# A perceiver block: the maximum of a softmax found in 32x32 blocks on VectorE and one small transposition on TensorE

## The chip, the core and the metric

The kernel runs on one core of a Trainium2 chip. TensorE (PE) multiplies matrices into PSUM, VectorE (DVE) and ScalarE (ACT) work elementwise, GpSimd (POOL) adds and issues some loads, SyncE (SP) issues the others. The metric is the device time of one launch in microseconds, a median of several runs; less is better. Granted TensorE clock in the profiled execution: 1.000.

## What is computed

Eight batches of 64 latent rows of 512 pass through cross attention on a context of 1601 rows of 256 per batch (16 heads of 128), causal self attention, and a gated feed-forward layer with ternary weights, each with a residual. The change lies in the softmax of the cross attention:

```python
q = (hidden_states @ Wq).reshape(B, Sq, H, D)
k = (encoder_hidden_states @ Wk).reshape(B, Skv, H, D)
v = (encoder_hidden_states @ Wv).reshape(B, Skv, H, D)
q = rmsnorm(q, gq)
k = rmsnorm(k, gk)
scores = jnp.einsum('bqhd,bkhd->bhqk', q, k) * scale
attn = jax.nn.softmax(scores, axis=-1)
out = jnp.einsum('bhqk,bkhd->bqhd', attn, v)
```

With `B` = 8, `Sq` = 64, `Skv` = 1601, `H` = 16, `D` = 128.

## The kernel before

**Units.** The cross attention is cut into 16 units: unit `u` is one batch and one half of the heads (8 heads of 64 queries, so 512 columns, `W`). Scores lie with the keys on the partitions: 12 full tiles of 128 keys and a tail of 65, each 128 x 512. The keys are never projected for the scores: the query side is multiplied with the key weights ahead of the loop, and the context itself is the other factor. The projected keys are needed only for their norms: squares are summed, and each row of scores is scaled by the root.

**Steps.** A unit has six steps, `step(u, q)`, q from 0 to 5, with two key tiles each (a pair). The projected keys and the scores of a pair come from a 2x2 block scheme with seven products instead of eight. `p_u` (tag "k" in PSUM), `p_5` and `p_2` (tag "m") are banks of key products; `s_a` and `s_2` (tag "s") those of scores. `c12`, `c22` and `c11` are sums that VectorE makes out of banks (L963, L981, L1010); ScalarE squares them (L684). The last product of a step into `p_u` overwrites what `c22` has read.

**One unit behind.** While unit `u` makes its scores, unit `u - 1` goes through its softmax: in step 0 its maximum is found, in steps 1 to 4 `less_max` subtracts it on VectorE, `exponentials` runs on ScalarE, `add_to_sums` on GpSimd; `weigh` (L775, `y`) multiplies the exponentials with the context, two tiles per step and three in step 1, three tiles later still (`LAG`); `finish` (L802) divides by the sums in the step in which the last of these products ends. In the first unit that has a predecessor, step 0 has nothing to weigh. `later` holds the scaling of the pair before, with its running maximum (`scale_pair`, L654 and L670), which is run early in the next step.

**The maximum.** `mx[u]`, 128 x 512, holds for every partition the maximum over the 13 tiles. `find_max` turns it on TensorE in four 128x128 transpositions into a bank of tag "m" (`tp_mx`, L733) and reduces over the free axis (L735): `m`, 128 x 4, one maximum per column. To put it on all partitions `spread_diag` splits it into two fp32r parts (L703, L705) and multiplies the identity with each (`dg`, 128 x 512, L709); `spread` sums the rows of both with a matrix of ones (`bp`, L110), and ScalarE copies the bank to `mB` (L727). In step 0 the first two are called behind the exponentials and ahead of `weigh(1)` and `product_7`; `spread_max` is called near the end of the step, behind the last score product.

**Order.** In the loop the order on PE, DVE, ACT and POOL is that of the calls (`tc.manual_schedule`). Behind the loop only PE keeps it; a scheduler orders the other engines. There the last unit's maximum is found, the first half of the values is projected (`values`, `vp`, L846), its exponentials are taken and weighed (`y`).

**Buffers.** Tiles of a tag share that tag's buffers: "t2" has 12 buffers of 128 x 512, "m", "k" and "s" two PSUM banks each.

Of the kernel before, what the change touches and what calls it, by code (L numbers as in the profile page):

```python
# [9 lines left out]
F32 = mybir.dt.float32  # L10
BF = mybir.dt.bfloat16

FR = mybir.dt.float32r
AF = mybir.ActivationFunctionType
ALU = mybir.AluOpType
AX = mybir.AxisListType
# [3 lines left out]
P = 128  # L20
# [8 lines left out]
def perceiver_kernel(  # L29
# [18 lines left out]
    nc = tc.nc  # L48
# [7 lines left out]
    HG = H // G  # L56
# [10 lines left out]
    W = HG * S  # L67
# [11 lines left out]
    small = ctx.enter_context(tc.tile_pool(name="small", bufs=4))  # L79
# [4 lines left out]
    ident = const.tile([P, P], F32, name="ident")  # L84
# [22 lines left out]
    def sum_rows(out_, parts):  # L107

        for i, part in enumerate(parts):
            nc.tensor.matmul(  # L110
                out_, ones_r, part, start=(i == 0), stop=(i == len(parts) - 1)
            )

    def moments(src, t):
# [467 lines left out]

    def quantise(u, aw, sg):

        tot = small.tile([P, 8], F32, tag="tot", name="tot")
        nc.vector.tensor_reduce(tot, aw, AX.X, ALU.add)
        scl = small.tile([P, 8], BF, tag="scl", name="scl")
        nc.vector.tensor_scalar(scl, tot, 1.0 / 64, SCALE_MIN, ALU.mult, ALU.max)

        thr = small.tile([P, 8], F32, tag="thr", name="thr")  # L590
        nc.vector.tensor_scalar(thr, scl, 257.0 / 512, None, ALU.mult)
        m = fq.tile([P, 8, 64], BF, tag="m", name="m")
        nc.vector.tensor_tensor(
            m, aw, thr.unsqueeze(2).to_broadcast([P, 8, 64]), ALU.is_gt
        )
        nd = fq.tile([P, 8, 64], BF, tag="nd", name="nd")
        nc.vector.tensor_tensor(
            nd, aw, scl.unsqueeze(2).to_broadcast([P, 8, 64]), ALU.subtract
        )
        return u, m, nd, aw, sg  # L600
# [71 lines left out]
    def bank(name, tag="m"):  # L672
        return ps.tile([P, 4 * HD], F32, tag=tag, name=name)
# [4 lines left out]
    def product(out_, a, w, start):  # L678

        nc.tensor.matmul(out_, a, w, start=start, stop=True, skip_group_check=not start)  # L680
# [15 lines left out]
            load_context(u, j)  # L696
            n_cx += 1

    def spread_diag(col):


        hi = small.tile([P, W // P], FR, tag="chi", name="chi", bufs=2)
        nc.vector.tensor_copy(hi, col)  # L703
        lo = small.tile([P, W // P], FR, tag="clo", name="clo", bufs=2)
        nc.vector.tensor_tensor(lo, col, hi.bitcast(F32), ALU.subtract)  # L705
        dg = []
        for part in (hi, lo):
            d = work.tile([P, W // P, P], FR, tag="t2", name="dg", bufs=12)
            nc.vector.tensor_tensor(  # L709
                d,  # L710
                ident.unsqueeze(1).to_broadcast([P, W // P, P]),
                part.bitcast(F32).unsqueeze(2).to_broadcast([P, W // P, P]),
                ALU.mult,
            )
            dg.append(d.rearrange("p a k -> p (a k)"))
        return dg

    def spread(parts):

# [4 lines left out]
    def spread_max(u):  # L724
        bp = spread(mB[u])
        mB[u] = work.tile([P, HG, S], F32, tag="t2", name="mB", bufs=12)
        nc.scalar.copy(mB[u].rearrange("p h s -> p (h s)"), bp)  # L727

    def find_max(u):
        tp = bank("tp_mx").rearrange("p (i k) -> p i k", k=P)  # L730
        flat = mx[u].rearrange("p h s -> p (h s)")
        for i in range(W // P):
            nc.tensor.transpose(tp[:, i, :], flat[:, ts(i, P)], ident)  # L733
        m = small.tile([P, W // P], F32, tag="m4", name="m4")
        nc.vector.tensor_reduce(m, tp, AX.X, ALU.max)  # L735
        mB[u] = m

    def tiles_of(u, js):
# [25 lines left out]
    def weigh_context(u, j):  # L764
        b, g = divmod(u, G)
        r = rows(j)
        if j == 0:
            yps[u] = [
                ps.tile([P, HG, S], F32, tag=f"y{c}", name=f"y{c}", bufs=1)
                for c in range(NC)  # L770
            ]
        s = s_sb.pop((u, j))
        s_pair.pop((u, j // 2), None)
        for c in range(NC):
            nc.tensor.matmul(  # L775
                yps[u][c],
                cxn[u, j][:r, ts(c, P)],
                s[:r],
                start=(j == 0),
                stop=(j == NJ - 1),  # L780
            )
# [16 lines left out]
    def finish(u):  # L798

        b, g = divmod(u, G)  # L800
        for c in range(NC):
            nc.vector.tensor_tensor(  # L802
                a_sb[g][c][:, :, ts(b, S)], yps[u][c], rB[u], ALU.mult
            )
# [37 lines left out]
    def values(h, tag):  # L842
        g, hg = divmod(h, HG)
        vp = ps.tile([P, NT], F32, tag=tag, name="vp")
        for c in range(NC):
            nc.tensor.matmul(  # L846
                vp,
                wv_sb[g][:, c, ts(hg, HD)],
                a_sb[g][c][:, hg, :],
                start=(c == 0),  # L850
                stop=(c == NC - 1),
            )
        if g == 0:
            o_sb[h] = work.tile([P, NT], F32, tag="og", name="o_h", bufs=HG)
        else:
            o_sb[h] = work.tile([P, NT], F32, tag="t2", name="o_h", bufs=12)
        (nc.scalar.copy if h % 2 else nc.vector.tensor_copy)(o_sb[h], vp)
# [24 lines left out]
    def weigh(k):  # L882
        nonlocal n_av
        for _ in range(k):
            if n_av >= 0:
                load_contexts(n_av + CXN)
                weigh_context(*divmod(n_av, NJ))
                if n_av % NJ == NJ - 1:
                    finish(n_av // NJ)
            n_av += 1  # L890

    def step(u, q):
# [14 lines left out]

        p_u = bank("p_u", "k")
        product(p_u, a11, b11, True)
        for js in probs[:1]:  # L910
            less_max(u - 1, js)
        if u > 0 and q == NQU - 1 and halves:
# [17 lines left out]
            less_max(u - 1, js)  # L930
        while later:
            later.pop(0)()

        n_early = 1 if q == 4 else 0
        for js in probs[:n_early]:
# [35 lines left out]
            for j in js:  # L971
                add_to_sums(u - 1, j, nc.gpsimd)

        if u > 0 and q == 0:
            find_max(u - 1)
            mB[u - 1] = spread_diag(mB[u - 1])
        c22 = kept("c22")

        def product_7():
# [2 lines left out]

        if u > 0 and q != 1:
            weigh(1)
        if q == NQU - 1 and n_q - 1 in quantised:
            put_by(n_q - 1)
        if u > 0 and q == NQU - 1:
# [16 lines left out]
        product(s_a[:, 1], s3, v3, False)  # L1004
        product(s_a[:, 0], s4, q22, False)
        nc.vector.tensor_tensor(quarters[:, 1::2], s_a, half[:, 0:2], ALU.add)  # L1006
        p_2 = bank("p_2")
        product(p_2, a12, b21, True)
        c11 = kept("c11")
# [7 lines left out]
        product(s_2, a12, q21, True)  # L1017
        nc.vector.tensor_tensor(quarters[:, 0], s_2, half[:, 2], ALU.add)
        product(s_a[:, 1], a22, m4, False)
        if u > 0 and q == 0:  # L1020
            spread_max(u - 1)
        nc.scalar.copy(quarters[:, 2], s_a[:, 1])
        if halves:
            signed(*halves.pop())
# [37 lines left out]
    with tc.manual_schedule(engines={mybir.EngineType.PE}):  # L1062

        later.pop()()
        wv_sb.append(load_wv(1))
        for jw in range(NJ - LAG, NJ):
            load_contexts((last - 1) * NJ + jw + CXN)
            weigh_context(last - 1, jw)
        find_max(last)
        mB[last] = spread_diag(mB[last])  # L1070
        finish(last - 1)
        for h in range(HG // 2):
            values(h, "k")
        spread_max(last)
        for h in range(HG // 2, HG):
            values(h, "k")
        x_sb = wkv.tile([P, NTT, D], F32, tag="w", name="x_again")
        nc.gpsimd.dma_start(x_sb, xf.rearrange("(t p) d -> p t d", p=P))
        for j in range(NJ):
            less_max(last, (j,))  # L1080
            exponentials(last, (j,))
            add_to_sums(last, j, nc.vector)
        n_wo = 0
        for j in range(NJ):
            load_contexts(last * NJ + j + CXN)
            weigh_context(last, j)
            if j == NJ - 3:
                find_sum(last)
            if j == NJ - 2:
                spread_sum(last)  # L1090
                for i in range(4):
                    invert_sums(last, i)
        for h in range(H):
            load_wo(h)
        wa_qk = big.tile([P, ND, 2 * D], F32, tag="A", name="wa_qk")
        nc.gpsimd.dma_start(
            wa_qk, w_attn[:, 0 : 2 * D].rearrange("(c p) n -> p c n", p=P)
        )
        wa_vp = big.tile([P, 2, ND, D], F32, tag="A", name="wa_vp")
        nc.gpsimd.dma_start(  # L1100
            wa_vp[:, 0], w_attn[:, 2 * D :].rearrange("(c p) n -> p c n", p=P)
        )
        nc.gpsimd.dma_start(wa_vp[:, 1], w_aproj.rearrange("(c p) n -> p c n", p=P))
        finish(last)


        x1 = x_sb
        ops = {0: ps.tile([P, D], F32, tag="s", name="op")}
        project(ops[0], 0, range(HG))
        for h in range(HG, H):  # L1110
            values(h, "k")
# [487 lines left out]
```

## Time and profile before

| what | us |
|---|---|
| median of 3 runs (1689.68 to 1690.12) | 1689.89 |
| the profiled execution | 1689.57 |
| its span, first to last instruction | 1687.8 |
| first and last start of `tp_mx` | 206.7 and 1398.0 |
| from one unit's `tp_mx` to the next (602.74 to 682.37) | 79.63 |
| `tp_mx`: 64 matmul records, one | 0.273 |
| L735, reduction of `tp_mx`: 16, one | 0.691 |
| L709, `dg`: 32, one | 0.684 |
| `bp` from `dg`: 32 records, one | 0.488 |
| `mB`, ScalarE's copy: 16, one | 0.578 |

Times of instructions count from the start of the span. A record of a matmul reaches beyond the start of the next, since matmuls are pipelined: the distance of two starts is what TensorE gives to one. In an order of time, a line with "x4" merges four instructions that follow each other, and brackets at its end give the engine's idle time before it and what ended that.

### The profile page before, as it was taken

The numbers are of one execution on the slowest core, as the hardware profiler recorded it, in microseconds if no ns is written. First come the engines' busy times: TensorE is split into PE (matmuls) and PEld (weight loads), VectorE is DVE, ScalarE is ACT, GpSimd is POOL, SyncE is SP. The second block draws the span as 40 slices with busy tenths as digits, with TensorE's granted clock in tenths as the row PEclk, the third lists the DMA queues.
The fourth block names the chain that finished last, engine by engine and source line by source line (L and its number), as shares of the span: only waits on it lengthen the run. The fifth ranks groups of instructions, "written<-read, shape, count | busy, mean of one in ns | idle before, by whom it ended". The sixth has DMA issues, their size and how long they took to land.

```text
span 1687.8 us, 20130 instructions
## 1 busy us (share of the span) xinstructions
PE 1668.6 (99%) x5472; PEld 953.1 (56%) x5472; DVE 1194.6 (71%) x1918; ACT 1155.2 (68%) x4511; POOL 448.1 (27%) x590
## 2 busy tenths in 40 slices
PE   7999899999999999999999999999999999999999
PEld 4665455555555555555555555555555554466787
DVE  4446878787888778787878787878788786245541
ACT  4667787878787877777777878787878773023441
POOL 3211232324232323232322323242324122100040
PEclk9999999999999999999999999999999999999999
DMA  6001122212221222222222222121221216500330
GB/s 200 16 0 36 33 52 45 48 39 50 49 52 36 45 47 49 48 43 47 43 49 47 44 46 47 40 57 43 46 43 37 63 30 238 156 1 1 100 101 25
DMA packets 255977, 92.61 MB, mean 55 GB/s; under 512 B 210144, under 2 KB 236536, under 8 KB 255864
## 3 DMA queue, kind: packets, MB, share of 16 engines
q1 hardware_dynamic: 246426, 69.04, 18.3%
q0 software_dynamic: 8864, 22.02, 4.4%
q8 instruction: 43, 0.70, 0.2%
q14 instruction: 70, 0.57, 0.1%
q10 hardware_dynamic: 574, 0.27, 0.1%
HBM read 77.62 MB, written 7.34 MB: 50 GB/s over the span
## 4 chain that ended last, share of the span: by engine, by line
PE 94%; ACT 3%; DVE 2%; DMA 1%; issue 0%; SPq 0%; DVEq 0%; ACTq 0%
PE y L775 21%; PE p_u L680 19%; PE s_a L680 14%; PE p L680 14%; PE gu L1414 4%; PE op L861 3%; PE s L680 2%; PE fop L1528 2%; PE mm_qk L1209 2%; PE aps L484 2%; PE vp L846 2%; PE sp L633 2%; PE q_u L388 2%; PE kp L266 1%; PE q L388 1%; ACT c L684 1%
## 5 line engine op out<-in xcount | busy, mean ns | idle before, releaser
L684 ACT ACTIVATE c<-c 128x128 f32<-128x128 f32 x1152 | 340.6, 297 | 143.4 <-DVE c L981 57.7
L775 PE MATMUL y<-s,cxn 128*128 128x512 f32 x768 | 356.6, 592 | 0.0
L775 PEld LDWEIGHTS y<-s,cxn 128*128 128x128 f32 x768 | 144.6, 190 | 151.2 <-issue 137.0
L684 ACT ACTIVATION_READ_ACCUMULATOR c<-c 128x1 f32 x1152 | 215.4, 187 | 0.0
L762 POOL TENSOR_TENSOR den<-den,s 128x512 f32<-128x512 f32 x150 | 190.7, 1271 | 43.4 <-ACT s L753 36.4
L680 PEld LDWEIGHTS s_a<-aT,cxS 128*128 128x128 f32 x576 | 109.3, 190 | 138.0 <-issue 126.8
L969 POOL COPY gate<-mx 128x1 f32<-128x1 f32 x60 | 11.0, 183 | 619.0 <-DVE mx L668 287.6
L680 PE MATMUL s_a<-aT,cxS 128*128 128x256 f32 x576 | 171.4, 379 | 0.0
L654 DVE TENSOR_TENSOR s<-s,ssq 128x1024 f32<-128x1024 f32 x96 | 117.2, 1221 | 25.4 <-ACT ssq L105 25.3
L753 ACT ACTIVATE s<-s,zero_t 128x1024 f32<-128x1024 f32 (+1 forms) x117 | 115.9, 991 | 4.6 <-DVE s L749 4.6
L670 DVE TENSOR_TENSOR mx<-mx,s 128x512 f32<-128x512 f32 x160 | 113.6, 710 | 7.5
L749 DVE TENSOR_TENSOR s<-s,mB 128x1024 f32<-128x1024 f32 (+1 forms) x117 | 116.4, 1017 | 2.2 <-ACT mB L727 2.1
L981 DVE TENSOR_TENSOR c<-p_u,p 128x512 f32<-128x512 f32 x96 | 64.9, 676 | 71.6 <-PE p_u L680 71.6
L1006 DVE TENSOR_TENSOR s<-s_a,half 128x512 f32<-128x512 f32 x96 | 66.1, 688 | 58.1 <-POOL den L762 40.7
L684 ACT ACTIVATE p_u<-p_u 128x128 f32<-128x128 f32 x384 | 99.9, 260 | 9.4
L680 PE MATMUL p_u<-wkS,cxT 128*128 128x512 f32 x192 | 98.7, 595 | 2.3 <-DVE c L981 2.3
L680 PE MATMUL p_u<-wkS,cxS 128*128 128x512 f32 x192 | 98.3, 594 | 1.5 <-ACT p L917 1.5
L680 PE MATMUL p<-wk,cxS 128*128 128x512 f32 x192 | 98.4, 594 | 0.0
L680 PE MATMUL p<-wkS,cxS 128*128 128x512 f32 x192 | 98.1, 592 | 0.0
L680 PE MATMUL p<-wk,cxT 128*128 128x512 f32 x192 | 98.0, 592 | 0.0
L680 PE MATMUL p_u<-wk,cxS 128*128 128x512 f32 x192 | 98.0, 592 | 0.0
L680 PE MATMUL p_u<-wk,cxT 128*128 128x512 f32 x192 | 98.0, 592 | 0.0
(232 smaller groups left out, 3248.4 us busy)
## 6 DMA issues: line engine op xcount, KB each, us to landing
cxn<-in_ctx_dram SPq DMA_DIRECT2D x192, 128.0 KB
cxB<-in_ctx_dram SPq DMA_DIRECT2D x192, 64.0 KB
wf<-in_L_ffn_w_gate_up_dram SPq DMA_DIRECT2D x32, 256.0 KB
fgu<-fw POOLq DMA_DIRECT2D x4, 2048.0 KB, 8.9
fw<-wT SPq DMA_DIRECT2D x192, 32.0 KB
wq<-in_L_xattn_Wq_dram SPq DMA_DIRECT2D x4, 1024.0 KB
wf<-in_L_ffn_w_proj_dram SPq DMA_DIRECT2D x16, 256.0 KB
wo<-in_L_xattn_Wo_dram POOLq DMA_DIRECT2D x16, 256.0 KB, 6.9
```

The costliest lines, as they stand in the source:

```text
L388: nc.tensor.matmul(out_, a[:, c], b[:, c], start=first, stop=True, skip_group_check=not first)
L654: nc.vector.tensor_tensor(flat, flat, kr.unsqueeze(2).to_broadcast([P, 2 * HG, S]), ALU.mult)
L670: nc.vector.tensor_tensor(mx[u][:r], mx[u][:r], s[:r], ALU.max)
L680: nc.tensor.matmul(out_, a, w, start=start, stop=True, skip_group_check=not start)
L684: nc.scalar.activation(k[:, ts(h, HD)], k[:, ts(h, HD)], AF.Square, accum_out=ssq[:, 4 * half + h : 4 * half + h + 1],)
L749: nc.vector.tensor_tensor(t, t, m.to_broadcast([r, len(js), W]), ALU.subtract)
L753: nc.scalar.activation(t, t, AF.Exp, bias=zero_t[: t.shape[0]], scale=1.0)
L762: eng.tensor_tensor(den[u][:r], den[u][:r], s[:r], ALU.add)
L775: nc.tensor.matmul(yps[u][c], cxn[u, j][:r, ts(c, P)], s[:r], start=(j == 0), stop=(j == NJ - 1),)
L981: nc.vector.tensor_tensor(c22, p_u, p5, ALU.add)
L1006: nc.vector.tensor_tensor(quarters[:, 1::2], s_a, half[:, 0:2], ALU.add)
L1414: nc.tensor.matmul(gu[:, cols], fgu_sb[rr // 8][:, rr % 8, c, :], xs_[n_][c][:, cols], start=(c == 0 and n_ == 0), stop=(c == ND - 1 and n ...
```

## The change

1. **Maxima in blocks.** A new function `turn_max` transposes `mx[u]` in 32x32 blocks on VectorE (`mxT`) and reduces over the inner 32 (`colmax`, 128 x 16): partition 32i + a, column j now holds the maximum of column 32j + a over the key rows 32i to 32i + 31. It is called in step 0 right behind the scaling of the last pair. `find_max` turns this 128 x 16 tile in one transposition, and reduces over i with a strided view: `m` is 16 x 32, kept in the first part of `mxT`.
2. **A smaller diagonal.** `spread_diag` multiplies the 16x16 identity with the parts, so `dg` is 16 x 512 and the sum over rows contracts 16 partitions. It is a generator now: the part `hi` is made at once, `lo` behind the step's second score addition (L1006 before).
3. **Calls.** `find_max` and the first part of `spread_diag` move behind `weigh(1)`. `spread_max` moves from the end of step 0 into step 1, behind its first product.
4. **Behind the loop**: `turn_max`, then `finish` of the unit before, one projection of values, and only then `find_max`; the spread comes behind five projections instead of four.
5. Some small buffers have fewer copies (`tot` two, `chi` and `colmax` one).

```diff
     def quantise(u, aw, sg):
-        tot = small.tile([P, 8], F32, tag="tot", name="tot")
+        tot = small.tile([P, 8], F32, tag="tot", name="tot", bufs=2)
...
-    def spread_diag(col):
-        hi = small.tile([P, W // P], FR, tag="chi", name="chi", bufs=2)
-        nc.vector.tensor_copy(hi, col)
-        lo = small.tile([P, W // P], FR, tag="clo", name="clo", bufs=2)
-        nc.vector.tensor_tensor(lo, col, hi.bitcast(F32), ALU.subtract)
+    NW = W // 32
+
+    def spread_diag(m):
+        hi = small.tile([P, 32], FR, tag="chi", name="chi", bufs=1)[:NW]
+        nc.vector.tensor_copy(hi, m)
+        nc.vector.tensor_tensor(m, m, hi.bitcast(F32), ALU.subtract)
         dg = []
-        for part in (hi, lo):
-            d = work.tile([P, W // P, P], FR, tag="t2", name="dg", bufs=12)
+        for part in (hi.bitcast(F32), m):
+            d = work.tile([P, NW, 32], FR, tag="t2", name="dg", bufs=12)[:NW]
             nc.vector.tensor_tensor(
                 d,
-                ident.unsqueeze(1).to_broadcast([P, W // P, P]),
-                part.bitcast(F32).unsqueeze(2).to_broadcast([P, W // P, P]),
+                ident[:NW, :NW].unsqueeze(2).to_broadcast([NW, NW, 32]),
+                part.unsqueeze(1).to_broadcast([NW, NW, 32]),
                 ALU.mult,
             )
             dg.append(d.rearrange("p a k -> p (a k)"))
-        return dg
+            yield dg
...
+    def turn_max(u):
+        t = work.tile([P, NW, 32], F32, tag="t2", name="mxT", bufs=12)
+        nc.vector.transpose(
+            t.rearrange("p j k -> p (j k)"), mx[u].rearrange("p h s -> p (h s)")
+        )
+        cm = small.tile([P, NW], F32, tag="cm", name="colmax", bufs=1)
+        nc.vector.tensor_reduce(cm, t, AX.X, ALU.max)
+        colmax[u] = cm, t
+
     def find_max(u):
-        tp = bank("tp_mx").rearrange("p (i k) -> p i k", k=P)
-        flat = mx[u].rearrange("p h s -> p (h s)")
-        for i in range(W // P):
-            nc.tensor.transpose(tp[:, i, :], flat[:, ts(i, P)], ident)
-        m = small.tile([P, W // P], F32, tag="m4", name="m4")
-        nc.vector.tensor_reduce(m, tp, AX.X, ALU.max)
+        tp = bank("tp_mx")[:NW, :P]
+        cm, t = colmax.pop(u)
+        nc.tensor.transpose(tp, cm, ident)
+        m = t[:NW, 0]
+        nc.vector.tensor_reduce(
+            m, tp.rearrange("j (i a) -> j a i", a=32), AX.X, ALU.max
+        )
         mB[u] = m
...
         p_u = bank("p_u", "k")
         product(p_u, a11, b11, True)
+        if u > 0 and q == 1:
+            spread_max(u - 1)
         for js in probs[:1]:
             less_max(u - 1, js)
...
         while later:
             later.pop(0)()
+            if u > 0 and q == 0:
+                turn_max(u - 1)
...
-        if u > 0 and q == 0:
-            find_max(u - 1)
-            mB[u - 1] = spread_diag(mB[u - 1])
         c22 = kept("c22")
...
         if u > 0 and q != 1:
             weigh(1)
+        diag = iter(())
+        if u > 0 and q == 0:
+            find_max(u - 1)
+            diag = spread_diag(mB[u - 1])
+            next(diag)
...
         nc.vector.tensor_tensor(quarters[:, 1::2], s_a, half[:, 0:2], ALU.add)
+        for dg in diag:
+            mB[u - 1] = dg
         p_2 = bank("p_2")
...
         product(s_a[:, 1], a22, m4, False)
-        if u > 0 and q == 0:
-            spread_max(u - 1)
...
-        find_max(last)
-        mB[last] = spread_diag(mB[last])
-        finish(last - 1)
-        for h in range(HG // 2):
+        turn_max(last)
+        finish(last - 1)
+        values(0, "k")
+        find_max(last)
+        for dg in spread_diag(mB[last]):
+            mB[last] = dg
+        for h in range(1, HG // 2 + 1):
             values(h, "k")
         spread_max(last)
-        for h in range(HG // 2, HG):
+        for h in range(HG // 2 + 1, HG):
             values(h, "k")
```

`sum_rows` takes as many rows of the ones as its part has partitions.

## The prediction

> **What bounds the kernel now.** I read the busy line and the chain first, then TensorE's waits, then single units in order of time. The page:
>
> ```profile
> PE 1668.6 (99%) x5472; PEld 953.1 (56%) x5472; DVE 1194.6 (71%) x1918; ACT 1155.2 (68%) x4511; POOL 448.1 (27%) x590
> ...
> PE 94%; ACT 3%; DVE 2%; DMA 1%; issue 0%; SPq 0%; DVEq 0%; ACTq 0%
> ```
>
> TensorE is busy 99% of the span and is 94% of the chain. Busy records of matmuls overlap, so this alone could hide slack. Two units in windows (length, then busy time of PE, PEld, DVE, ACT, POOL) and TensorE's waits in the loop and at its end (us in total, times, longest) settle it:
>
> ```profile
> 602.74:682.37 79.63, 79.63 (x235) 43.40 (x233) 64.42 (x100) 62.29 (x257) 24.57 (x32) 1.00 0.22 46
> 206.68:284.18 77.50, 76.89 (x224) 41.77 (x225) 62.04 (x98) 61.58 (x256) 23.87 (x32) 1.00 0.24 47
> ```
>
> ```profile
> PE p_u L680 <- DVE c L981: 2.3, 3, 1.3
> PE p_u L680 <- ACT p L917: 1.5, 3, 0.7
> PE tp_mx L733 <- DVE mx L670: 0.9, 2, 0.7
> ```
>
> A later unit has no idle TensorE time at all; the first with a maximum (206.68) has some. The waits are eight in all, and in order of time they stand at or before 216 us and at 1397, none in units 2 to 15. So there every microsecond of TensorE taken away is a microsecond of the unit, as long as nothing new makes it wait; VectorE has 15 us idle per unit, ScalarE 17.
>
> **The transpositions and their true price.** The chain in order of time, at one unit:
>
> ```profile
> 682.37 0.44 PE tp_mx L733 x4
> 682.81 1.72 PE y L775 x4
> 684.53 0.86 PE p_u L680 x2
> ...
> 688.83 0.46 PE bp L110 x2
> ```
>
> Four transpositions hold TensorE 0.44 us from the first start to the next matmul (0.109 each by the trace's starts, which stand 0.16 before the chain's stamps), though each has a record of 273 ns. Three go: 0.327 us per unit. There are 16 (64 records by 4).
>
> The Trainium skill (TensorE: Matmul & The Clock Gate, "Part 4: PE-mode transpose") gives about 275 ns for one in a kernel's context. The record agrees, the spacing does not; by the page 48 would be worth 13.2 us and the kernel would take 1676.7 us, an estimate; I go by the spacing.
>
> The one transposition left is new in form (16 columns of weights): its bounds are 0 and its record, 0.273; I take 0.109, as its moving side is the same 128x128. That leaves -1.7 to +2.6 us over 16. The spread's matmuls now contract 16 rows: rows of 65 and of 128 partitions both take 592 ns (y L775), 32-row ones 284 against 273 of 128-row ones, all records that may cover for each other; I take no change. Their place (behind p_u of the next step) costs TensorE nothing by itself.
>
> **VectorE's added work.** A 32x32 transposition 128x512 f32: 0.694 (L194). A reduction of 512 f32 from SBUF: 0.684 (L275). The reduction out of PSUM shrinks from 512 to 128 elements, read with a stride: between 0.17 (the 128x4 cast) and 0.69 (the old one); I take 0.29, the 128x130 copy out of PSUM (L512). The two small ones grow from 4 to 32 elements, 0.17 to 0.20. The two dg stay 512 long: 0.68. Net +1.04 us per unit, 16.6 in all, beside TensorE's work if slack holds. The same unit on VectorE:
>
> ```profile
> 680.46 1.42 DVE L670 TENSOR_TENSOR mx<-mx,s 128x512 f32<-128x512 f32 x2
> 682.05 0.69 DVE L963 TENSOR_TENSOR c<-p,u 128x512 f32<-128x512 f32 x1 [0.17 <-PE p L680]
> 682.85 0.69 DVE L735 TENSOR_REDUCE m<-tp_mx 128x4 f32<-128x512 f32 x1
> ...
> 685.43 0.69 DVE L981 TENSOR_TENSOR c<-p_u,p 128x512 f32<-128x512 f32 x1 [0.28 <-PE p_u L680]
> ```
>
> The Trainium skill speaks against it (VectorE: DVE Perf Modes, "Rules for kernel authors"): TensorE for a 128x128 transposition, and a reduction on a hot path should be restructured away. No row here shows VectorE as the hot path; were its 16.6 us on it, the sum would be 1689.6 - 5.2 + 16.6 = 1701 us, an estimate.
>
> Now the queue, in this unit's times. TensorE runs the y matmuls in the transpositions' place, 682.21 to 683.93, then the one transposition, and everything behind is 0.33 earlier. On VectorE:
> - mx ends 681.88; transposition to 682.61, reduction to 683.33. TensorE asks for it at 683.93: 0.55 spare.
> - Behind them stands c12 (L963), now 683.25 to 683.94, 1.2 late. ScalarE's squares wait for it: with the abs and sign behind them they end at 686.30 instead of 685.09, which uses up the 1.06 that ScalarE idled before the c22 squares.
> - The transposition's record ends 684.20; reduction 684.24 to 684.53, cast to 684.76, dg hi (it need not wait for lo) 684.88 to 685.56. Behind it c22 (L981), 685.48 to 686.17. TensorE's product into the same bank wants c22 released at 686.95 - 0.33 = 686.62: 0.40 spare, after 0.05 for the release. This is the tightest place.
> - dg lo is put off behind the s_a addition, so c11 ends 687.97 instead of 687.84; ScalarE starts its squares 0.12 late and keeps that to the step's end. mB is now copied after s: 690.9 to 691.5 instead of to 691.11, so less_max starts at 691.52 instead of 691.14. Queued behind it are finish, the next less_max, the scaling, c12 and c22. Exponentials want the first at 694.64 (done 692.75), the new y bank wants finish at 696.1 (done 693.9), the p_u product wants p1 at 693.10 (done 691.98). All have 1 us or more.
>
> SP's and POOL's order stay as they are; TensorE's loads of context hang on its own progress. So the 14 steady units give 14 x 0.327 = 4.58 us.
>
> **The two ends give some back.** In the first unit with a maximum no y matmuls exist to cover the new chain:
>
> ```profile
> 206.68 0.66 PE L733 MATMUL tp_mx<-ident,mx 128*128 128x128 f32 x4 [0.68 <-DVE mx L670]
> ...
> 215.55 1.12 PE L680 MATMUL p_u<-wkS,cxS 128*128 128x512 f32 x2 [0.20 <-ACT p L917]
> ```
>
> mx ends at 206.63, so colmax at 208.07 and the transposition starts 208.12, 1.44 late. c12 comes at 208.68; ScalarE's squares, abs and sign end at 210.93; c11 at 212.32, so its squares start 212.35 instead of 211.50, and ScalarE runs without a gap from there to p1, for which TensorE waited until 215.55. It now waits to 216.39: +0.84, saving included.
>
> At the end (the last unit):
>
> ```profile
> 1397.58 1.28 DVE L802 TENSOR_TENSOR a<-y,rB 128x512 f32<-128x512 f32 x2
> ...
> 1397.71 0.66 PE L733 MATMUL tp_mx<-ident,mx 128*128 128x128 f32 x4 [0.23 <-DVE mx L670]
> 1398.31 7.13 PE L846 MATMUL vp<-a,wv 128*128 128x512 f32 x16
> ```
>
> The built order puts the new transposition between the two halves of finish. The first value's matmuls start at 1398.31 as before (on the first half), but the second half now ends at 1399.49 and they stall until 1399.54; its end and the transposition come at 1400.55, the other 14 matmuls and the spread at 1413.03 instead of 1412.61: +0.42. The exponentials, then from 1409.4, stay ahead.
>
> **Sum.** -4.58 + 0.84 + 0.42 = -3.3 us. The profiled execution (1689.57, of which the span is 1687.8 and 1.8 lies around it) becomes 1686.3, its span 1684.5. The median shown, 1689.89, is 0.3 above that execution, so I say 1686.6. A measurement of this kernel tells 0.2% from no change, 3.4 us, a limit at 1686.5: the forecast lies on it.
>
> **Rivals.**
> - *The ends cost nothing* (the first unit's stall is taken up, the last one's order is kind): 16 x 0.327 = 5.2, 1684.7. For it: ScalarE's small idles elsewhere. Against: the first unit already waits at three places, one behind the other.
> - *c22 comes late in every unit.* Strided PSUM reading and 16-row operations have no row. If the reduction, cast and subtraction each cost the 512-element 0.69, dg hi starts at 686.29 instead of 684.88 (0.40 and 0.49 for two of them, 0.52 for the third, behind which it stands at the 0.60 spacing of such operations). c22 then ends at 687.58, TensorE stalls 1.0 per unit, net +0.67 x 14 = 9.4, first unit 0.84 + 1.36, end 0.42: 1702. It decides from 0.40 of delay on; at 0.64 the whole gain is gone (14 x 0.24 = 3.3). For it: the tightest slack. Against: 16x512 has the same length as a row known at 0.68, and the cast would have to triple.
> - *A small stall in each unit*, 0.1 to 0.2, at c22 or at the transposition: 1688 to 1689.4.
> - *The change doesn't do what it says*: TensorE's spacing at one lone transposition is its whole record: +2.6, 1689.2; or the records were the price: 48 x 0.273 = 13.1 less, 1676.8.
>
> **How the numbers follow.** Forecast 0.60 (own range 1685.8 to 1687.6; 0.26 of it under 1686.5, the rest within 0.2%), free ends 0.14 (faster), small stall or lone record 0.12 (no change), c22 late 0.12 (slower in the main), cheap records 0.01. Faster 0.41, same 0.47, slower 0.12. The range leaves out the far part of the late c22 and a little below: 1684.6 to 1690.2.
>
> **What would show it.** Distance between transpositions of neighbouring units 79.27 to 79.30 instead of 79.6; TensorE's wait for VectorE at tp_mx or p_u absent in units 2 to 15; a wait near 208 for colmax of 2 us and one for p1 near 216; c12 1.2 us later behind the reduction; near 1399 a wait of the value product for finish. Wrong would make it: a recurring wait of p_u for c22, or the small reduction above 0.6.

## The result, and the profile after

The change made the kernel slower, by 0.2%. The median is 1692.91 us (20 runs, 1690.79 to 1694.28) against 1689.35 us before (20 runs, 1686.85 to 1690.83): ratio 1.0022, 95% interval 1.0015 to 1.0029. The profiled execution took 1693.14 us, its span is 1691.4 us. The prediction said 1686.6, with a range from 1684.6 to 1690.2.

The page of the changed kernel, busy time and shares of the chain:

```profile
PE 1672.0 (99%) x5424; PEld 945.8 (56%) x5424; DVE 1210.3 (72%) x1950; ACT 1154.3 (68%) x4511; POOL 447.4 (26%) x590
...
PE 94%; ACT 2%; DVE 2%; DMA 1%; issue 0%; SPq 0%; DVEq 0%; ACTq 0%
```

48 matmuls fewer, and TensorE is busy 3.4 us longer. VectorE has the added 16 us, and its share of the chain stays at 2%. Windows of one later unit and of the first with a maximum (length, then busy time of PE, of PEld, which is TensorE's loading of weights, of DVE, ACT and POOL, then the granted clock, the busy share of the DMA engines and their GB/s):

```profile
606.44:686.10 79.66, 79.66 (x230) 42.86 (x229) 65.31 (x101) 62.21 (x257) 24.42 (x32) 1.00 0.22 46
208.09:287.81 79.72, 79.72 (x226) 42.98 (x227) 63.81 (x100) 62.03 (x258) 23.81 (x32) 0.98 0.23 46
```

The later unit still shows no idle TensorE time, and is not 0.33 us shorter but 0.05 longer (79.66 against 79.61, the median over the units). The first unit shows a mean granted clock of 0.98, where the same unit before had 1.00. TensorE's waits (us in total, times, longest):

```profile
PE tp_mx L751 <- DVE colmax L745: 2.1, 1, 2.1
PE p_u L684 <- DVE c L1002: 1.9, 2, 1.3
PE p_u L684 <- ACT p L939: 1.3, 2, 0.7
PE vp L866 <- DVE a L822: 0.8, 1, 0.8
```

No wait comes back in every unit; `tp_mx` waits once, in the first unit. So the steady units lose time in TensorE's own stream. The chain in order of time tells where (start, duration, what); before, the two `bp` took 0.46 and four `y` 1.72:

```profile
686.27 0.11 PE tp_mx L751
686.38 0.86 PE p_u L684 x2
...
690.68 0.86 PE p_u L684 x2
691.54 0.66 PE bp L110 x2
692.20 1.91 PE y L795 x4
```

The lone transposition costs 0.11, as forecast. The two matmuls of the spread take 0.20 more, and the `y` products behind them 0.19 more: 0.39 us per unit, which eats the 0.33.

In the first unit with a maximum, TensorE in order of time (start, length, line, shapes, idle time ahead and its end):

```profile
205.35 0.59 PE L684 MATMUL s_a<-aT,cxS 128*128 128x256 f32 x2
208.09 0.28 PE L751 MATMUL tp_mx<-ident,colmax 128*16 128x128 f32 x1 [2.15 <-DVE colmax L745]
208.21 1.26 PE L684 MATMUL p_u<-wk,cxS 128*128 128x512 f32 x2
209.26 1.06 PE L684 MATMUL s_a<-aT,cxS 128*128 128x256 f32 x2
```

The same stretch in windows (columns as above):

```profile
203.00:205.90 2.90, 2.53 (x6) 0.97 (x6) 1.94 (x3) 2.27 (x6) 0.00 (x0) 1.00 0.35 36
205.90:208.60 2.70, 0.55 (x3) 0.31 (x3) 2.63 (x5) 0.37 (x1) 0.00 (x0) 1.00 0.09 10
208.60:212.50 3.90, 3.90 (x9) 2.23 (x8) 2.99 (x8) 3.49 (x18) 0.00 (x0) 0.56 0.00 0
```

The forecast wait is there. In the window behind it the mean granted clock is 0.56 over 3.9 us, and `s_a` takes 1.06 where it took 0.59. By the trace's record of the clock it is 0.50 from 208.87 to 212.28 and 1.00 around that.

To account for the span, both traces are cut at the same matmuls:

| stretch | before | after | difference |
|---|---|---|---|
| start to the `p_u` ahead of the first `tp_mx` | 203.41 | 203.37 | -0.04 |
| from there to the first `y` | 15.41 | 17.36 | +1.95 |
| to the first `y` of a tail (65 rows) | 73.14 | 73.11 | -0.03 |
| 14 units on, to the last one in the loop | 1103.64 | 1104.59 | +0.95 |
| to the first `y` behind the loop | 17.00 | 17.84 | +0.84 |
| to the end | 275.18 | 275.11 | -0.07 |

Rows are start to start, except the last. The sum is +3.60, the difference of the spans up to rounding. The first row varies between executions by itself (200.97 to 203.58 in the ten traces), so kernels with a single run are read below by these stretches and by the distance of neighbouring `tp_mx` (the median over the steady units), not by their times.

### The profile page after: what moved, and what is told of

It reads as the page before. It is cut to its first block, busy times and chain, and to the rows that moved or that the text cites. A ratio compares the mean times of both kernels' runs of the same rounds, so it can differ in the third digit from the quotient of the medians.

```text
span 1691.4 us, 20068 instructions
## 1 busy us (share of the span) xinstructions
PE 1672.0 (99%) x5424; PEld 945.8 (56%) x5424; DVE 1210.3 (72%) x1950; ACT 1154.3 (68%) x4511; POOL 447.4 (26%) x590
## 4 chain that ended last, share of the span: by engine, by line
PE 94%; ACT 2%; DVE 2%; DMA 1%; issue 0%; SPq 0%; DVEq 0%; ACTq 0%
PE y L795 21%; PE p_u L684 19%; PE s_a L684 14%; PE p L684 14%; PE gu L1443 4%; PE op L881 3%; PE s L684 2%; PE fop L1557 2%; PE mm_qk L1238 2%; PE aps L488 2%; PE sp L637 2%; PE vp L866 2%; PE q_u L392 2%; PE kp L270 1%; PE q L392 1%; PE bp L110 1%
```

## The experiments

The first theory: with 16 rows the weights of a matmul are no longer loaded behind the matmul before it. The rival: the new place, between `p_u` and the 65-row products, does it. Besides: what the clock and VectorE's queue have to do with the first unit.

### 128 rows in the identity part

```diff
-            d = work.tile([P, NW, 32], FR, tag="t2", name="dg", bufs=12)[:NW]
+            d = work.tile([P, NW, 32], FR, tag="t2", name="dg", bufs=12)[:P]
...
-                ident[:NW, :NW].unsqueeze(2).to_broadcast([NW, NW, 32]),
-                part.unsqueeze(1).to_broadcast([NW, NW, 32]),
+                ident[:P, :NW].unsqueeze(2).to_broadcast([P, NW, 32]),
+                part.unsqueeze(1).to_broadcast([P, NW, 32]),
```

`hi` and `m` have 128 rows too.

> The two matmuls that spread the maximum contract 128 rows again (the identity part is zero below row 16); their place, the number of instructions and everything else stay as in the changed kernel, and the result is the same. Theory (few rows): with 16 rows the weights of a matmul are not brought in behind the matmul before it, and that costs 0.39 us at the two spreads' matmuls of each unit. Then the distance between the maximum transpositions of neighbouring units falls from 79.66 to 79.27 us, the two bp matmuls start 0.23 us apart instead of 0.34, and the time falls by 16 x 0.39 = 6.2 us, from 1692.9 to 1686.7. Rival (place): the cost comes from standing behind p_u and ahead of the 65-row products. Then the distance stays at 79.66 and the time at 1692.9.

Measured: 1686.31 us (11 runs) against 1688.75 before on the same chip (21 runs), ratio 0.9985, interval 0.9976 to 0.9993. The distance of neighbouring `tp_mx` is 79.27, and TensorE still has no idle time in a unit:

```profile
604.75:684.02 79.27, 79.27 (x230) 43.01 (x229) 65.39 (x101) 62.09 (x257) 24.61 (x32) 1.00 0.23 46
```

The chain of this kernel:

```profile
688.60 0.86 PE p_u L684 x2
689.46 0.46 PE bp L110 x2
689.92 1.72 PE y L795 x4
```

0.46 and 1.72 again, in the new place. TensorE's weight loads in order of time (start, duration), first of the changed kernel:

```profile
690.30 0.41 PEld L684 LDWEIGHTS p_u<-wk,cxT 128*128 128x128 f32 x2
691.47 0.29 PEld L110 LDWEIGHTS bp<-dg,ones_r 16*128 16x128 f32 x2 [0.76 <-PE s_a L684]
692.12 0.30 PEld L795 LDWEIGHTS y<-st,cxn 65*128 65x128 f32 x2 [0.37 <-issue]
```

And of this one:

```profile
688.87 0.19 PEld L110 LDWEIGHTS bp<-dg,ones_r 128*128 128x128 f32 x1 [0.24 <-PE s_a L684]
689.30 0.19 PEld L110 LDWEIGHTS bp<-dg,ones_r 128*128 128x128 f32 x1 [0.24 <-DVE tot L590]
689.53 0.42 PEld L795 LDWEIGHTS y<-st,cxn 65*128 65x128 f32 x2
```

With 128 rows the load for `bp` starts together with the second `p_u` matmul (688.87), behind which it is hidden. With 16 rows that matmul starts at 690.95 and gives way at the usual 0.43, at 691.37; the load starts only at 691.47, 0.09 later, and the record of `bp` with it. The `y` behind shows the same at 692.12. Within the pair the second load starts 0.11 behind the first, ahead of its own matmul (691.81).

### 16 rows, spread back at the end of the first step

```diff
-        if u > 0 and q == 1:
-            spread_max(u - 1)
...
         product(s_a[:, 1], a22, m4, False)
+        if u > 0 and q == 0:
+            spread_max(u - 1)
```

> The changed kernel with its 16-row matmuls, but with the spread called at the end of step 0 again, where the kernel before had it. Theory (few rows): the cost goes along, 79.66 us from unit to unit, time about 1692.9. Rival (place): the cost is gone, 79.27 us and 1686.7. If the weights in front of the 65-row products play a part as well, something between.

Measured: 79.69 from unit to unit, 1694.46 us (one run). The chain:

```profile
691.22 0.66 PE bp L110 x2
691.88 1.05 PE p_u L684 x2
692.93 1.72 PE y L795 x4
```

The cost went along: 0.20 at `bp` and 0.19 at what stands behind it, now `p_u` (1.05 instead of 0.86); the 65-row `y` is back at 1.72. The place is not the cause.

### 64 and 65 rows

The edit is that of the first experiment, with 64 or 65 for `P`.

> As the first run of this group, with 64 rows instead of 128 in the identity part. If any contraction that fills less than the array keeps its weights from being brought in early: 79.66 us as with 16 rows. If only the small 32-row tile that the program gives a 16-row matmul does it: 79.27 us. If the cost grows as rows are missing: near 79.48. The rival (place) expects 79.66 here as well as with 128 rows.

> As the run with 128 rows, with 65 rows in the identity part, one more than the 64 that showed the full cost (79.69 us from unit to unit). The y products, which contract 65 rows, stand beside 128-row matmuls at the usual 429 ns. Theory (switch): the cost belongs to a change between a matmul that the program gives the whole array and one that it gives a smaller tile of it (64 rows or fewer), so 65 rows cost nothing: 79.27 us, bp 0.23 us apart. Rival (fewer rows cost more, by degrees): between 79.3 and 79.69, near 79.6.

Measured: 64 rows 79.69 (1690.38 us, one run), 65 rows 79.27 (1686.20, one run). The chain with 64 rows:

```profile
688.11 0.67 PE bp L110 x2
688.77 1.91 PE y L795 x4
```

The chain with 65 rows:

```profile
688.25 0.46 PE bp L110 x2
688.72 1.72 PE y L795 x4
```

Full cost or none, between two neighbouring row counts: no cost by degrees. The step fits the theory that a matmul of up to 64 rows gets a smaller tile, a part of the array, and one of 65 rows the whole, like its neighbours; the tile itself stands in no trace.

### Two changes of size more

```diff
+        if u > 1 and q == 1:
+            spread_half(u - 1)
         p_u = bank("p_u", "k")
         product(p_u, a11, b11, True)
         if u > 0 and q == 1:
             spread_max(u - 1)
```

`spread_half` issues the first of the two matmuls of the spread, `spread_max` then only the second.

> The changed kernel with 16 rows, but the first of the two spread matmuls goes ahead of the first product of the second step and the second stays behind it (the first unit with a maximum is left as it was), so that TensorE changes from 128-row to 16-row matmuls and back four times instead of twice in a unit; same number of matmuls, same result. Theory (switch, about 0.2 us each way and back, since within the pair the second one's weights are brought in early): the distance from unit to unit rises by 0.39, from 79.66 to 80.05 us, the time by 13 x 0.39 = 5 us. Rival (each 16-row matmul costs 0.2 wherever it stands): 79.66 and no change.

Measured: 80.05 from unit to unit, as the theory of the switch said, and 1695.55 us (one run); the stretch of 14 units is 1109.65 against 1104.59 in the changed kernel, the 5 us forecast. The chain:

```profile
689.15 0.42 PE bp L734
689.57 1.06 PE p_u L684 x2
690.62 0.43 PE bp L739
691.05 1.92 PE y L805 x4
```

The pair now takes 0.85 instead of 0.66, `p_u` 1.06 instead of 0.86, `y` 1.92 as it was: the same two matmuls, but 0.39 more for one more pair of switches. Over the kernel with 128 rows (79.27), one pair of switches costs 0.39 and two cost 0.78, so nothing is left for the 16-row matmul as such; the way to the few rows and the way back cost 0.2 each. How much of that is waiting for the matmul before and how much the load that is not hidden was not separated.

### The first unit: transposition behind more products

```diff
-        if u > 0 and q == 0:
+        if u > 1 and q == 0:
             find_max(u - 1)
...
         nc.vector.tensor_tensor(quarters[:, 1::2], s_a, half[:, 0:2], ALU.add)
+        if u == 1 and q == 0:
+            find_max(0)
+            diag = spread_diag(mB[0])
```

> Only in the first unit that has a maximum (which has no products to weigh) the transposition and the identity parts come behind product_7, the s_a products and the s_a addition, so that TensorE does not stand for 2.15 us ahead of the transposition; all other units as in the changed kernel. Theory (clock): the idle stretch lowered the granted clock to 0.56 for 3.9 us, and that is the 1.1 us by which this unit lost more (1.96) than was worked out (0.84). Then no window near 208 to 212 us shows a clock under 0.95, matmuls there stay 216 ns apart, and the time is about 1.1 us less, 1691.8; up to 2.0 less if the wait itself is covered too. Rival (VectorE's queue): the block transposition and reduction ahead of c12 make ScalarE late whatever TensorE does, so the lost time comes back as waits of p_u for p1 or c22 near 210 to 217 us, and the time stays within 0.4 of 1692.9.

Measured: 1691.52 us (11 runs), ratio to before 1.0013, interval 1.0004 to 1.0022. TensorE there, in order of time:

```profile
207.90 0.28 PE L751 MATMUL tp_mx<-ident,colmax 128*16 128x128 f32 x1 [0.42 <-DVE colmax L745]
...
216.13 1.13 PE L684 MATMUL p_u<-wkS,cxS 128*128 128x512 f32 x2 [1.35 <-ACT p L939]
```

The window in which the changed kernel had a clock of 0.56 (here the clock is 1.00; the 0.56 behind it is the share of the DMA engines):

```profile
208.60:212.50 3.90, 3.90 (x12) 2.00 (x12) 3.83 (x10) 3.78 (x21) 0.00 (x0) 1.00 0.56 105
```

Both theories hold for a part. The lowered clock is gone, and the stretch from `p_u` to the first `y` is 1.14 us shorter than in the changed kernel (16.22 against 17.36), where 1.1 was forecast. The rest stays: 16.22 us against 15.41 before, +0.81, now as a wait for `p1`, ScalarE's copy of the bank `p_u` (1.35, before 0.20), because the block transposition and reduction stand ahead of c12 in VectorE's queue; in the last experiment they do not, and the wait is gone.

The lowered clock does not come in every execution. The run with 64 rows has the same 2.15 us of idle time, and its clock stayed up. The traces' record of the clock tells these executions apart. In all ten traces the clock changes only at whole multiples of 3.413 us from its first rise (in the changed kernel it drops after 57 of them and comes back after 58), so time falls into periods of 3.413 us. In the changed kernel the whole idle time lies in one period, and the clock is 0.50 in the next one (windows laid on the periods):

```profile
205.45:208.87 3.42, 1.27 (x6) 0.59 (x5) 3.28 (x7) 0.58 (x2) 0.00 (x0) 1.00 0.11 12
208.87:212.28 3.41, 3.41 (x7) 2.02 (x6) 2.54 (x6) 3.28 (x18) 0.00 (x0) 0.50 0.00 0
```

With 64 rows the border of two periods, 205.16, cuts the idle time (203.55 to 205.70) in two:

```profile
201.74:205.16 3.42, 1.81 (x5) 0.67 (x4) 3.28 (x5) 1.55 (x4) 0.00 (x0) 1.00 0.30 30
205.16:208.57 3.41, 2.87 (x10) 1.81 (x11) 3.34 (x8) 2.29 (x11) 0.00 (x0) 1.00 0.00 0
```

Of the seven traces with this idle time five show the drop (stretch to the first `y`: 17.36 to 17.77) and two do not (16.22 and 16.23). In the five, the period ahead of the drop held 2.10 to 2.15 us of idle TensorE time; in the two, no period there held more than 1.61. Why the periods stand differently to the program each time no run shows. By the mean granted clock of the runs, 14 of 20 of the changed kernel are at 0.999 (median 1693.45) and 6 at 1.000 (1692.03); with the idle time cut to 0.42, all 11 are at 1.000.

### Behind the loop: finish ahead of the block transposition

```diff
-        turn_max(last)
         finish(last - 1)
+        turn_max(last)
```

> Only behind the loop: the sums of the unit before are finished ahead of the block transposition instead of behind it. If VectorE's order there is what makes the values' matmuls wait near 1402 us (0.23 us seen), that wait goes and the stretch from the last y products to the first exponentials' end shortens by 0.2 to 0.4 us. If the transposition to TensorE then waits for VectorE instead, the wait stands at tp_mx and nothing is gained.

Measured: 1692.04 us (one run). TensorE in this kernel, in order of time:

```profile
1399.56 1.98 PE L866 MATMUL vp<-a,wv 128*128 128x512 f32 x4 [0.82 <-DVE a L822]
1401.50 0.28 PE L751 MATMUL tp_mx<-ident,colmax 128*16 128x128 f32 x1
```

The first four matmuls hold TensorE 1.94 us (start to the next start) instead of 2.16 in the changed kernel and 1.72 unhindered: half of the stall is gone, and `tp_mx` does not wait. The stretch to the first `y` behind the loop falls from 17.84 to 17.68, less than the 0.2 to 0.4 expected, and the one to the tail's `y` 21 us later is the same (38.98 and 38.96). The order is worth 0.16 at its place; what takes it back later was not tried.

### All together

128 rows, the order of the run before, and in the first unit:

```diff
-            if u > 0 and q == 0:
+            if u > 1 and q == 0:
                 turn_max(u - 1)
...
         nc.vector.tensor_tensor(quarters[:, 1::2], s_a, half[:, 0:2], ALU.add)
+        if u == 1 and q == 0:
+            turn_max(0)
...
         product(s_a[:, 1], a22, m4, False)
+        if u == 1 and q == 0:
+            find_max(0)
+            for dg in spread_diag(mB[0]):
+                mB[0] = dg
```

> All in one: 128 rows in the identity part, the order behind the loop of the run before this one, and in the first unit with a maximum the block transposition behind the s_a addition and the rest of the maximum at the end of step 0, so that neither VectorE's c12 and c22 nor TensorE waits for it. By the terms: 15 distances of 79.27 instead of 79.60 give 4.9 us, the first unit gives 0.3 and shows no lowered clock and no wait for p1 over 0.3, the end loses 0.2 or nothing: 1683.5 to 1684.5 where the kernel before has 1688.75, a ratio of 0.997. If the first unit's loss only moves to another wait (less_max for mB, or p1 as before), 1685.5.

Measured: 1683.26 us (6 runs, 1682.45 to 1685.06) against 1688.78 before (10 runs), ratio 0.9968, interval 0.9956 to 0.9980; all runs at clock 1.000. A later unit and the first one in windows:

```profile
599.88:679.18 79.30, 79.30 (x230) 43.02 (x229) 65.44 (x101) 62.11 (x257) 24.71 (x32) 1.00 0.22 46
207.86:282.76 74.90, 73.99 (x213) 39.44 (x211) 61.46 (x97) 59.04 (x245) 24.22 (x32) 1.00 0.24 48
```

TensorE in the first one, in order of time:

```profile
207.86 0.27 PE L751 MATMUL tp_mx<-ident,colmax 128*16 128x128 f32 x1
...
209.79 1.10 PE L110 MATMUL bp<-dg,ones_r 128*128 128x512 f32 x2 [0.80 <-DVE dg L715]
```

The stretch of the first unit is 14.54 against 15.41 before. A new wait that was not forecast, 0.80 of `bp` for the identity part, stands there, and the gain of 0.87 is larger than the 0.3 forecast all the same: the three waits of before (0.68 for `mx`, 0.41 for c22, 0.20 for `p1`) are gone. At the end the stretch to the first `y` is 17.30 against 17.00, a loss of 0.3 where 0.2 was expected at most. This version beats both kernels.

## Why the prediction was wrong

**The step that failed** is "The spread's matmuls now contract 16 rows: ... I take no change." It cost 0.39 us per unit where 0.33 was to be won. The step compared records (592 with 592, 284 with 273), and records do not decide this: a record says how long one matmul lasts in a stream of its kind, not what a change between kinds costs, and the 65-row `y` used as a witness lies on the free side of the step between 64 and 65 rows. The same prediction had shown for the transpositions that record and spacing differ. 0.39 x 14 = 5.5 us, of which 0.95 shows as a loss and the rest ate the gain. The Trainium skill has the rule (TensorEngine Tiling (Array Packing), "Key Properties"): a change of the tiling mode drains TensorE. It was not weighed in the prediction. The runs fit it, though no trace shows the mode, and they give the change a price here: 0.39 us for going to 16 or 64 rows and back, 0.20 of it at the small matmuls and 0.19 behind them.

**Right:**
- What bounds the kernel: no idle TensorE time in the steady units, before and after.
- The price of the transpositions: three times 0.109. With the switch out of the way the distance falls from 79.61 to 79.27, 0.34 for the 0.327 forecast. The rivals that charge or pay whole records fall.
- "Their place ... costs TensorE nothing by itself": the spread moved back, the cost stayed.
- VectorE in the steady units, as the trace of the changed kernel shows it:

```profile
684.09 0.71 DVE L741 STREAM_TRANSPOSE mxT<-mx 128x512 f32<-128x512 f32 x1
684.84 0.69 DVE L745 TENSOR_REDUCE colmax<-mxT 128x16 f32<-128x512 f32 x1
685.44 0.68 DVE L987 TENSOR_TENSOR c<-p,u 128x512 f32<-128x512 f32 x1
686.41 0.28 DVE L753 TENSOR_REDUCE mxT<-tp_mx 16x32 f32<-16x128 f32 x1 [0.29 <-PE tp_mx L751]
```

The reduction out of PSUM takes 0.28 (0.29 assumed, 0.17 to 0.69 the bounds). c12 stands behind the reduction and harms nobody. The rival that c22 comes late in every unit falls: the 1.9 us that `p_u` waits for it are two waits in all.

**Right in mechanism, off in size:**
- The first unit, +0.84 forecast. The transposition started at 208.09 (208.12 forecast), and in executions without the drop of the clock the stretch is +0.81 and +0.82. The profiled execution has +1.95; the drop adds 1.1 to 1.6 in the five traces that have it. It was a second thing that the prediction left out: the wait near 208 was charged as a wait alone, and the idle times of 0.7 us there before showed no drop.
- The end, +0.42. With 128 rows the stretch to the first `y` behind the loop is 17.45 against 17.00, +0.45. The changed kernel has 17.84, another 0.39 for the switch there and back.

So the sum of the prediction without its failed step stands: with 128 rows, all else as in the change, the kernel took 2.4 us less than before (interval 1.2 to 4.1), where 3.3 was forecast, and 7 of these 11 runs are at a mean clock of 0.999. The rival of *a small stall in each unit* (0.1 to 0.2, at c22 or at the transposition) is not what happened either: the loss is larger, and no engine waits; the time goes inside TensorE. The rival that the ends cost nothing falls by the two stretches above. Two slips of the prediction change nothing: its five chances add up to 0.99, and its "other 14 matmuls" at the end are 28, as its times count them.

## What to carry to other kernels

In a stream that TensorE bounds, look out for single matmuls that contract few rows among full ones: padding a contraction of 16 rows with zeros to the size of its neighbours cost nothing, and one pair of 16-row matmuls between full ones lost more than three removed transpositions won. Read the price of a matmul from the distance of starts at the very neighbours it will have, and the weight loads' starts for whether they are hidden. Where a pipeline fills, look at the idle stretch a longer chain makes for TensorE: it can cost twice, as a wait and as clock.

## What the hardware showed unexpectedly

- The price of a contraction has a step: 64 rows cost 0.39 us per pair of switches, 65 rows nothing.
- An idle stretch of 2.15 us was followed by a granted clock of 0.50 for 3.41 us in five of seven traces, and by no drop in two. What tells them apart is whether the stretch lay, all but 0.05 us, in one period of 3.413 us of the clock's record (2.10 to 2.15 us idle in it: drop) or was cut in two (1.61 and 0.54, 1.59 and 0.57: none). The Trainium skill (TensorE: Matmul & The Clock Gate, "Why this matters for your kernels") warns of idle gaps over about 3 us; here a shorter one was enough in most executions. Its page calls the window in which the hardware watches TensorE free-running ("What's actually happening"); the periods in the traces, which stand differently to the idle time from execution to execution, agree.
